# A one-column constant tile widened from 4 to 64 bytes, in an attention and feed-forward block

## The chip, the core and the metric

The kernel runs on one core of a Trainium2 chip. A core has TensorE (PE, matrix multiplication), VectorE (DVE), ScalarE (ACT), GpSimd (POOL) and SyncE (SP, whose queue issues most of the DMAs). Operands stand in SBUF, which has 128 partitions; a tile takes the same byte range of every partition, so that its place is one start address. Results of multiplications go to eight PSUM banks. The metric is device time in microseconds, as the median of several executions.

## The reference

The input x has 2048 rows (tokens) of 1024 columns, in float32. Cut to what matters:

```python
def attn(x):                                   # one head of 256
    q, k, v = split(x @ Wqkv + bqkv)
    p = softmax(q @ k.T / 16)
    return (p @ v) @ Wo + bo

def ffn(x):                                    # 1024 -> 2752 -> 1024
    return (silu(x @ W_gate.T) * (x @ W_up.T)) @ W_down.T

x = x + layernorm(attn(layernorm(x)))
x = x + layernorm(ffn(layernorm(x)))
```

## The kernel before

Every multiplication is done in a split form: an operand is kept as a high and a low half of type float32r, and a product is the sum of three multiplications, high by high, high by low and low by high (mm3, lines 143 to 147, and mmc, lines 601 to 606, which holds line 604). Each loads a 128x128 block of weights from SBUF and streams 512 columns of a moving operand from SBUF past them, into a PSUM bank. The halves are made by split (lines 107 to 109): a cast on ScalarE (L108), then a subtraction on VectorE (L109).

The work goes through these stages.

1. *Projections and layernorm.* Rows of x are loaded by 128 (load_x, L163), normalised, transposed by TensorE against an identity tile called ident (L138) and split into xT, which is the tile xT0 or a2 in turn. qk (lines 184 on) multiplies xT by the weights wqk, and v_block (L205, L206) multiplies xT by the v weights, which are in wvo.
2. *Attention.* For each block of 128 rows: scores (through mm3, q as weights and kx as moving data; q is in qa or qb by turns of four blocks), softmax on ScalarE and VectorE, transposes of the probabilities p_s (turn, L267), the product with v (attend, L275 and L276, both operands in a1 and a2), a transpose of its result (turn_o, L284), the output projection (proj, through mm3, oTs as weights and wvo as moving data), the residual and the transposes for the feed-forward stage (xpose, L346).
3. *Feed forward, gate and up* (gate_up, lines 622 to 690). The tokens are taken in two halves. The products are arranged by a scheme of sums in the manner of Strassen, seven in place of eight. Moving data are the activations in xb, kx, a1, qa and qb. The weights are loaded into raw tiles (f2p, f4_4, wr0), combined on VectorE, split, and held in a ring of slots: four quarters of a2 and two halves of wvo. Which slot a weight gets depends on the order in which slots come free, so the same source line reads its weights from a2 at one time and from wvo at another. In the first half the remaining attention blocks' residual and transposes run as jobs between products.
4. *Feed forward, down* (run_down, run_steps). A slot holds both the weights and the moving data of a step, so that both operands are in a2, or both in wvo.

SBUF is given out from both ends. The pool "const" starts at the left end, at low addresses, and holds ident, the biases, the constant mhalf, the small statistics tiles ys and small, then a1, a2 and the raw tiles f4, f2p and f2_4; the pools "x0", "w", "s" and "xi" (xT0, wr, qb, p_s, oTs, xe, xi) stand behind it on the same side. Pools with side="right" are given out from the high end downwards:

```python
    rpool = pool("right", side="right")
    kx = tl(rpool, [P, 8, 2, 512], F32R, "kx")
    wvo = tl(rpool, [P, 4, 2, 512], F32R, "wvo")
    qa = tl(rpool, [P, 2, 2, 512], F32R, "qa")
```

wqk, xb and x1 are on the right as well. A tile's width in a partition is rounded up to 32 bytes. mhalf holds the exponent -0.5 for the reciprocal square root that GpSimd computes (L120, L804). The tile framework orders the instructions by a simulated timeline and sets the waits between engines.

Of the kernel before, what the change touches and what calls it, by code (L numbers as in the profile page):

```python
# [8 lines left out]
F32 = mybir.dt.float32  # L9
# [6 lines left out]
P = 128  # L16
# [18 lines left out]
def block_kernel(ctx, tc, x, wqk, wv, bqk, bv, wo, bo, wgu, wlast, wd, out):  # L35
# [14 lines left out]
    def pool(name, side=None, **kw):  # L50
        return tc.alloc_tile_pool(name=name, bufs=1, side=side, reuse_waits="tile", **kw)

    def tl(p, shape, dt, name):
        return p.tile(shape, dt, tag=name, name=name, bufs=1)


    cpool = pool("const")
# [2 lines left out]
    bqk_s = tl(cpool, [P, 4], F32, "bqk_s")  # L60
    bv_s = tl(cpool, [P, D], F32, "bv_s")
    bo_s = tl(cpool, [P, C], F32, "bo_s")
    mhalf = tl(cpool, [P, 1], F32, "mhalf")
    nc.vector.memset(mhalf, -0.5)

    ys = [tl(cpool, [P, 32], F32, f"ys{i}") for i in range(2 * TB)]
# [961 lines left out]
```

## Time and profile before

| what | value |
|---|---|
| median of 3 runs | 1729.71 us (1728.43 to 1729.87) |
| profiled execution | 1728.61 us, its span 1726.8 us |
| TensorE clock granted, mean | 0.992 |
| busy: TensorE, weight loads, VectorE, ScalarE, GpSimd | 1699.3, 1393.6, 1091.8, 689.1, 89.0 us |
| multiplications | 7788, 5424 of them at line 604 |
| feed-forward stage | from 454 us to the end of the span |
| DMA | 271.01 MB, 157 GB/s |

A group of the profile is the instructions of one line, engine and set of tiles, with the mean duration of one. Weight loads (PEld) overlap the multiplications. A multiplication's duration runs from its start to its modelled end, and the next starts before that; the distance from one start to the next is what it takes of TensorE's time. In tile names the buffer number is left out, so "a" is a1 or a2 and "f" is one of f4 and f2_4.

### The profile page before, as it was taken

To read this page: it belongs to the slowest core of one execution; us is meant where nothing else is said; L and a number is where in the kernel's file an instruction comes from. 1 tells how busy PE (TensorE), PEld (TensorE's weight loads), DVE (VectorE), ACT (ScalarE), POOL (GpSimd) and SP (SyncE) were. 2 spreads that over 40 slices of the span, in tenths; PEclk is the share of its full clock that TensorE was granted. 3 is DMA by queue.
4 is the path that set the end of the run, shared out by engine and by line. 5 is a ranking of instruction groups with operands and counts; after the bars stand their busy time and mean duration, and the time that the engine had idled before them with its cause. 6 is when DMAs were issued, how large, how long until landed. Compare 5 with 4: busy or idle time off the path is not lost.

```text
span 1726.8 us, 21119 instructions
## 1 busy us (share of the span) xinstructions
PE 1699.3 (98%) x7788; PEld 1393.6 (81%) x7788; DVE 1091.8 (63%) x1666; ACT 689.1 (40%) x1031; POOL 89.0 (5%) x118
## 2 busy tenths in 40 slices
PE   8999999999899999999999999999999999999997
PEld 7888887888688888888888888788888888888886
DVE  8633667667877777676378457866555564345458
ACT  3222445544544444443355444433333333244343
POOL 1000001000011111110000000100000000000001
PEclk8999999999899999999999999999999999999999
DMA  6221023234755566665358655633332223486654
GB/s 210 80 80 37 37 74 125 97 126 172 257 195 195 201 215 214 214 204 190 122 191 255 194 194 193 205 105 113 129 109 94 91 92 122 132 280 195 195 185 159
DMA packets 131015, 271.01 MB, mean 157 GB/s; under 512 B 13280, under 2 KB 29792, under 8 KB 130912
## 3 DMA queue, kind: packets, MB, share of 16 engines
q1 hardware_dynamic: 128176, 262.72, 45.6%
q10 hardware_dynamic: 2736, 6.95, 1.1%
q8 instruction: 61, 1.00, 0.2%
q14 instruction: 42, 0.34, 0.1%
HBM read 185.73 MB, written 83.89 MB: 156 GB/s over the span
## 4 chain that ended last, share of the span: by engine, by line
PE 93%; DVE 3%; DMA 2%; issue 1%; ACT 1%; POOL 0%; SPq 0%; POOLq 0%; DVEq 0%; ACTq 0%
PE bank L604 70%; PE bank L146 4%; PE bank L145 4%; PE bank L147 4%; PE bank L275 3%; PE bank L276 2%; PE bank L267 1%; PE bank L205 1%; PE bank L206 1%; PE bank L346 1%; DMA f<-x 1%; PE bank L138 1%; DVE small L115 0%; PE bank L773 0%; PE bank L774 0%
## 5 line engine op out<-in xcount | busy, mean ns | idle before, releaser
L604 PE MATMUL bank<-a 128*128 128x512 f32 x1176 | 273.8, 390 | 0.0
L604 PEld LDWEIGHTS bank<-a 128*128 128x128 f32 x1176 | 220.8, 188 | 46.8
L604 PE MATMUL bank<-xb,a 128*128 128x512 f32 x816 | 197.3, 395 | 0.0
L109 DVE TENSOR_TENSOR a<-f2p,a 128x1024 fp32r<-128x1024 f32 (+2 forms) x114 | 124.7, 1095 | 93.4 <-ACT a L108 81.0
L617 DVE TENSOR_TENSOR xi<-bank,xi 128x512 f32<-128x512 f32 (+1 forms) x168 | 113.3, 685 | 111.1 <-PE bank L604 70.1
L604 PEld LDWEIGHTS bank<-xb,a 128*128 128x128 f32 x816 | 152.9, 187 | 37.1
L604 PE MATMUL bank<-kx,a 128*128 128x512 f32 x648 | 157.1, 395 | 0.0
L604 PE MATMUL bank<-a,a 128*128 128x512 f32 x648 | 153.4, 390 | 0.0
L108 ACT CAST a<-f2p 128x1024 fp32r<-128x1024 f32 (+2 forms) x114 | 107.6, 949 | 112.5 <-PE bank L604 102.4
L109 DVE TENSOR_TENSOR a<-f,a 128x512 fp32r<-128x512 f32 (+3 forms) x93 | 91.3, 981 | 91.4 <-ACT a L108 88.0
L604 PEld LDWEIGHTS bank<-kx,a 128*128 128x128 f32 x648 | 121.5, 187 | 29.5
L604 PEld LDWEIGHTS bank<-a,a 128*128 128x128 f32 x648 | 121.6, 188 | 26.4
L604 PE MATMUL bank<-wvo 128*128 128x512 f32 x600 | 142.4, 390 | 0.0
L604 PEld LDWEIGHTS bank<-wvo 128*128 128x128 f32 x600 | 112.6, 188 | 24.4
L108 ACT CAST a<-f 128x512 fp32r<-128x512 f32 (+3 forms) x93 | 69.4, 747 | 125.7 <-PE bank L604 90.6
L275 PE MATMUL bank<-a,a 128*128 128x512 f32 x256 | 94.5, 402 | 2.8 <-ACT f L348 2.0
L109 DVE TENSOR_TENSOR wvo<-f2p,wvo 128x1024 fp32r<-128x1024 f32 (+2 forms) x48 | 54.8, 1141 | 66.2 <-ACT wvo L108 57.6
L604 PE MATMUL bank<-a,wvo 128*128 128x512 f32 x384 | 93.7, 396 | 1.2 <-ACT xi L663 1.2
L604 PE MATMUL bank<-kx,wvo 128*128 128x512 f32 x384 | 91.9, 390 | 0.0
L617 DVE TENSOR_TENSOR xi<-xi,xi 128x512 f32<-128x512 f32 x124 | 85.4, 688 | 4.3
L604 PEld LDWEIGHTS bank<-a,wvo 128*128 128x128 f32 x384 | 72.0, 188 | 18.8 <-ACT xi L663 1.6
L604 PEld LDWEIGHTS bank<-kx,wvo 128*128 128x128 f32 x384 | 72.1, 188 | 15.7
(234 smaller groups left out, 2751.2 us busy)
## 6 DMA issues: line engine op xcount, KB each, us to landing
f2p<-wgu SPq DMA_DIRECT2D x43, 512.0 KB, 5.0
hd_S<-xi SPq DMA_DIRECT2D x80, 256.0 KB, 4.6
f<-x SPq DMA_DIRECT2D x30, 512.0 KB, 3.9
hd_A<-xi SPq DMA_DIRECT2D x60, 256.0 KB, 2.0
f<-wgu SPq DMA_DIRECT2D x21, 512.0 KB, 4.4
wr<-wgu SPq DMA_DIRECT2D x20, 512.0 KB, 5.9
f<-wd SPq DMA_DIRECT2D x20, 512.0 KB, 5.0
td_T<-f SPq DMA_DIRECT2D x40, 256.0 KB, 4.5
```

What stands on the lines that cost most here:

```text
L108: nc.scalar.copy(hi, src)
L109: (lo_engine or nc.vector).tensor_tensor(lo, src, f32(hi), ALU.subtract)
L138: nc.tensor.transpose(b[:, j * P : (j + 1) * P], t[:, cb * P : (cb + 1) * P], ident)
L145: nc.tensor.matmul(o, w[0], m[0], start=first, stop=False)
L146: nc.tensor.matmul(o, w[0], m[1], start=False, stop=False)
L147: nc.tensor.matmul(o, w[1], m[0], start=False, stop=last)
L205: nc.tensor.matmul(b, xg[:, c, 0, cols], wv_s[:, c, :, :].rearrange("p a f -> p (a f)"), start=(c == 0), stop=False)
L206: nc.tensor.matmul(b[:, D:], xg[:, c, 1, cols], wv_s[:, c, 0, :], start=False, stop=(c == 7))
L275: nc.tensor.matmul(b, p[:, k, 0, :], vt[:, k, :, :].rearrange("p h d -> p (h d)"), start=(k == 0), stop=False)
L276: nc.tensor.matmul(b[:, D:], p[:, k, 1, :], vt[:, k, 0, :], start=False, stop=(k == NKB - 1))
L604: one = nc.tensor.matmul(o, w[i], m[j], start=first and n == 0, stop=last and n == 2, skip_group_check=chained)
L617: nc.vector.tensor_tensor(o, a, b, op)
```

## The change

The tile mhalf is made 16 columns wide, and its first column is used in its place. It is written and read as before.

```diff
-    mhalf = tl(cpool, [P, 1], F32, "mhalf")
+
+    mhalf = tl(cpool, [P, 16], F32, "mhalf")[:, 0:1]
     nc.vector.memset(mhalf, -0.5)
```

mhalf took 4 bytes, rounded up to 32, and takes 64 now. The tiles given out behind it on the left stand 32 bytes higher; those in front of it, and those on the right, stay. Some start addresses, in bytes within a partition:

| tile | side | before | modulo 64 | after | modulo 64 |
|---|---|---|---|---|---|
| ident | left, ahead of mhalf | 2176 | 0 | 2176 | 0 |
| bo_s | left, ahead of mhalf | 3744 | 32 | 3744 | 32 |
| mhalf | left | 7840 | 32 | 7840 | 32 |
| ys0 | left | 7872 | 0 | 7904 | 32 |
| a1 | left | 9920 | 0 | 9952 | 32 |
| a2 | left | 42688 | 0 | 42720 | 32 |
| f4_0 | left | 75456 | 0 | 75488 | 32 |
| qb | left | 114368 | 0 | 114400 | 32 |
| xb | right | 139232 | 32 | 139232 | 32 |
| kx | right | 172000 | 32 | 172000 | 32 |
| wvo | right | 204768 | 32 | 204768 | 32 |
| qa | right | 221152 | 32 | 221152 | 32 |

The blank line moves every later line number by one: line 604 is line 605 after it.

## The prediction

> **What bounds the kernel now.** I read the busy times first, then the chain that ended last, then the matrix multiplications grouped by the tiles they read, then the timeline of one stretch of the feed-forward stage. A residue below is a tile's start address in its partition modulo 64 bytes. In the built program every left tile from ys0 on has residue 0 before and 32 after; every right tile (kx, wvo, qa, xb, wqk, x1) has 32 in both; ident has 0 in both. A mixed multiplication reads moving data and weights of different residues, an equal one of the same. The tiles' inner steps are multiples of 64 bytes, so a slice has its tile's residue.
>
> ```profile
> PE 1699.3 (98%) x7788; PEld 1393.6 (81%) x7788; DVE 1091.8 (63%) x1666; ACT 689.1 (40%) x1031; POOL 89.0 (5%) x118
> PE 93%; DVE 3%; DMA 2%; issue 1%; ACT 1%; POOL 0%; SPq 0%; POOLq 0%; DVEq 0%; ACTq 0%
> ```
>
> TensorE is busy for 98% of the span and holds 93% of the chain, so nanoseconds on every multiplication reach the end. The groups (number left out of a name: "a" is a1 or a2, weights are in a2 or wvo; columns: line, engine, operation, tiles, tile size, count, busy us, mean ns):
>
> ```profile
> L604 PE MATMUL bank<-a 128*128 128x512 f32 x1176 | 273.8, 390 | 0.0
> L604 PE MATMUL bank<-xb,a 128*128 128x512 f32 x816 | 197.3, 395 | 0.0
> L604 PE MATMUL bank<-kx,a 128*128 128x512 f32 x648 | 157.1, 395 | 0.0
> L604 PE MATMUL bank<-a,a 128*128 128x512 f32 x648 | 153.4, 390 | 0.0
> L604 PE MATMUL bank<-wvo 128*128 128x512 f32 x600 | 142.4, 390 | 0.0
> L604 PE MATMUL bank<-a,wvo 128*128 128x512 f32 x384 | 93.7, 396 | 1.2 <-ACT xi L663 1.2
> L604 PE MATMUL bank<-kx,wvo 128*128 128x512 f32 x384 | 91.9, 390 | 0.0
> ```
>
> Left with left (a; a,a) and right with right (wvo; kx,wvo) take 390; the three that cross take 395 or 396. The code, the shape and the type are the same. Ends of multiplications are modelled, so I check it on starts (start us, us, engine, line, tiles, count):
>
> ```profile
> 501.95 5.77 PE L604 MATMUL bank<-kx,a 128*128 128x512 f32 x24
> 507.56 5.64 PE L604 MATMUL bank<-kx,wvo 128*128 128x512 f32 x24
> 513.04 5.63 PE L604 MATMUL bank<-a,a 128*128 128x512 f32 x24
> 518.51 5.76 PE L604 MATMUL bank<-a,wvo 128*128 128x512 f32 x24
> 524.10 11.36 PE L604 MATMUL bank<-xb,a 128*128 128x512 f32 x48
> 535.30 1.04 PE L346 MATMUL bank<-ident,f 128*128 128x128 f32 x8
> ```
>
> From one start to the next group's start, the mixed 24 + 24 + 48 take 5.61 + 5.59 + 11.20 = 22.40 us, 233.3 ns each; the equal 48 take 10.95 us, 228.1 ns each. A mixed multiplication costs 5.2 ns more, and both equal kinds (0 with 0, 32 with 32) are the cheap ones.
>
> **The change, part by part.** The scheduler's order does not move: each engine has the same instructions with the same waits, in the same places. One memset writes the same single column. All that changes is 32 bytes on the left tiles' addresses, after which left and right both have 32.
>
> *Feed-forward multiplications (L604).* Mixed now: 816 (xb,a), 648 (kx,a), 384 (a,wvo), and outside the rows above 180 (qa,a) and 60 (qb,wvo): 2088. All become equal. At 5.2 ns that is 10.9 us; by the rounded group means (5 to 6 ns) 10.4 to 12.5. I take 10.9. The multiplications that are equal already keep 390: residue 0 (a) and 32 (wvo) both have it.
>
> *Projections to q and k (qk).* 384 multiplications read xT (left) against wqk (right), all mixed, all becoming equal. No equal row of this line exists; its neighbours on the same source lines are the scores, in these rows:
>
> ```profile
> L145 PE MATMUL bank<-kx,qb 128*128 128x512 f32 x64 | 26.5, 415 | 0.0
> L145 PE MATMUL bank<-kx,qa 128*128 128x512 f32 x64 | 26.3, 411 | 0.0
> L147 PE MATMUL bank<-kx,qb 128*128 128x512 f32 x64 | 25.3, 396 | 0.0
> L147 PE MATMUL bank<-a,wqk 128*128 128x512 f32 x64 | 25.3, 395 | 0.0
> L147 PE MATMUL bank<-kx,qa 128*128 128x512 f32 x64 | 25.3, 395 | 0.0
> L346 PE MATMUL bank<-ident,f 128*128 128x128 f32 x112 | 15.5, 272 | 0.0
> ```
>
> Between 0 (as scores with qa, equal, against qb, mixed: 1 ns at L147) and 6 ns: 0 to 2.3 us. The layout of wqk and xT is that of the feed-forward operands and 395 is their mixed mean, so I take 5.2 ns: 2.0 us.
>
> *Scores with qb* (192, becoming equal): 0 to 1.2 us, by the rows about 1 ns: 0.2. *Output projection* (192, oTs left against wvo right): no equal row; 0 to 1.2, taken 1.0 as its contiguous moving operand is nearer to L604's. *v_block* (wvo moving, 128 of 512 and 128 of 256 columns): means of 393 and 282 lie under those of the equal attention products (402 and 286), so I take 0 from 0 to 1.3.
>
> *Transposes: the loss.* ident stays at 0 while every tile transposed against it moves from 0 to 32, so 128 (L138) + 128 (L346) + 256 (L267) + 32 (L284) = 544 equal ones become mixed. No mixed transpose exists before. Bounds: 0, and the 6 ns of a mixed 512-column product, 3.3 us in all. A transpose streams a quarter of the columns but loads as many weights; between those I take half of 5.2 ns: 1.4 us lost. In the stretch above one takes about 109 ns (the eight stand 0.87 us in the chain).
>
> *VectorE, ScalarE, DMA.* Their left operands move too. Rows with both kinds of destination:
>
> ```profile
> L109 DVE TENSOR_TENSOR a<-f2p,a 128x1024 fp32r<-128x1024 f32 x87 | 106.2, 1221 | 92.4 <-ACT a L108 80.5 <-PE bank L604 11.7
> L109 DVE TENSOR_TENSOR wvo<-f2p,wvo 128x1024 fp32r<-128x1024 f32 x41 | 50.0, 1220 | 66.1 <-ACT wvo L108 57.6 <-PE bank L604 8.5
> ```
>
> 1221 with all operands at 0, 1220 when they cross. The casts on ScalarE have 1053 (a) and 1045 (wvo): no price for 32. Loads of x_d into bo_s (residue 32) land in a median 4.3 us and into wr (0) in 4.0; of xT_d in 4.3 and 5.5: no direction, so 0. Were a transfer 0.3 us later, the cover is the ring of raw tiles loaded ahead; uncovered it would show at the start of the feed-forward stage, where the chain holds one load of 5.89 us.
>
> *Sum.* -10.9 - 2.0 - 0.2 - 1.0 + 1.4 = -12.7 us of TensorE time. The feed-forward part passes on: TensorE has 160.00 of 160 us from 775 and 443.47 of 444 from 1122. The front's net 1.8 us may be partly given back where TensorE waits (254.88 of 264 us from 190 to 454); I drop 0.4. That leaves 12.3. The profiled execution took 1728.6 (span 1726.8 and 1.8 around it): 1716.3. It lies 1.1 below the median 1729.7, so as a median 1717.4.
>
> **A rule against it.** The Trainium skill, SBUF — State Buffer, section "Who interferes with whom", gives TensorE two independent read ports, one for the moving operand and one for weight loads, and says TensorE never waits on anyone. By that rule the two operands' addresses could not matter and the sum would be 0. The trace disagrees with 390 against 395 ns.
>
> **Rivals.** (1) *Nothing changes.* The crossing price could belong to the two ends of the memory and not to the residue: in L604 the two always go together before. Then the 2088 still cross ends and keep 395, the transposes stay as they are, and the time is 1729.7. For: the scores show hardly any price. Against: nothing else in the code tells the two ends apart, and 32 bytes are the only difference their addresses share. (2) *The feed binds.* With faster products VectorE (240.59 of 321 us from 454 to 775) and DMA (0.61 there) might set the pace in the first half's gate and up products: eight periods of 108 mixed products (the 96 above and 12 of qa,a) are 4.5 us lost, 1721.9. Against: VectorE idles 25% there, and its waits are for TensorE. (3) *Slower.* A mixed transpose may lose its overlap with the next weight load. It decides at 12.3 + 1.4 = 13.7 us over 544, 25 ns on each of some 109. At 40 ns it costs 21.8 us and the time is 1739. For: weight loads are 81% of the span, short transposes have the least slack around them. Against: the mixed price seen is 5 ns a load, whatever the tile.
>
> **How the numbers follow.** Forecast 0.80, nothing 0.07, feed 0.07, slower 0.06. The unknown terms at their ends give gains of 12.5 + 2.3 + 1.2 + 1.2 + 1.3 = 18.5 (1711) and 10.4 - 3.3 = 7.1 (1722.6). All small terms at one end together is unlikely, so the low end is 1713; the high end is 1722.6, which holds the feed case. Outside are nothing and slower, 0.13, and a little below. About 0.2% (3.5 us) can be told from no change: faster has forecast and feed, 0.87; same 0.07; slower 0.06.
>
> **What would show it.** Right: every L604 group near 390; 24 products of kx,a or a,wvo from start to start in 5.48 us, not 5.6; L147 with wqk near 390; L346 between 272 and 278 ns, eight in 0.87 to 0.92 us; L109 still 1220. Wrong: xb,a and kx,a still at 395 (ends, not residues); xb,a at 390 with new idle time on TensorE released by casts (feed); transposes tens of ns longer (slower); or wvo and kx,wvo risen, if 32 was cheap only beside traffic at 0.

## The result and the profile after

The changed kernel takes 1708.58 us (1707.72 to 1712.36) beside 1729.26 us for the kernel before in the same measurement: a ratio of 0.9888, 95% interval 0.9876 to 0.9900. It is 1.1% faster, 20.7 us. The direction was the one forecast; the gain is 1.7 times the 12.3 us forecast, and the time lies 4.4 us below the low end of the range.

The profiled execution has a span of 1705.9 us, 20.9 less than before. Its busy times and chain by engine:

```profile
PE 1678.0 (98%) x7788; PEld 1393.6 (82%) x7788; DVE 1090.9 (64%) x1666; ACT 690.2 (40%) x1031; POOL 93.4 (5%) x118
PE 95%; DVE 2%; ACT 1%; issue 1%; DMA 1%; POOL 0%; POOLq 0%; DVEq 0%; ACTq 0%; SPq 0%
```

TensorE's busy time fell by 21.3 us, all of the gain; VectorE and ScalarE are within 1.1 us of what they were. The feed-forward groups (line 605 is the line 604 of before):

```profile
L605 PE MATMUL bank<-a 128*128 128x512 f32 x1176 | 272.7, 389 | 0.0
L605 PE MATMUL bank<-xb,a 128*128 128x512 f32 x816 | 192.0, 389 | 0.0
L605 PE MATMUL bank<-kx,a 128*128 128x512 f32 x648 | 152.9, 389 | 0.0
L605 PE MATMUL bank<-a,a 128*128 128x512 f32 x648 | 152.6, 389 | 0.0
L605 PE MATMUL bank<-wvo 128*128 128x512 f32 x600 | 141.5, 389 | 0.0
L605 PE MATMUL bank<-a,wvo 128*128 128x512 f32 x384 | 91.2, 389 | 1.2 <-ACT xi L664 1.2
```

The three crossing groups fell from 395 and 396, as forecast. But the groups that never crossed fell too, from 390 to 389. The starts in the timeline show it better, on the stretch that answers to the one shown before:

```profile
492.40 1.03 PE L347 MATMUL bank<-ident,f 128*128 128x128 f32 x8
493.19 1.62 PE L605 MATMUL bank<-qa,a 128*128 128x512 f32 x6
494.65 1.52 PE L605 MATMUL bank<-qb,a 128*128 128x512 f32 x6
496.01 1.52 PE L605 MATMUL bank<-qa,a 128*128 128x512 f32 x6
497.37 1.52 PE L605 MATMUL bank<-qb,a 128*128 128x512 f32 x6
498.73 5.60 PE L605 MATMUL bank<-kx,a 128*128 128x512 f32 x24
504.17 5.60 PE L605 MATMUL bank<-kx,wvo 128*128 128x512 f32 x24
509.61 5.60 PE L605 MATMUL bank<-a,a 128*128 128x512 f32 x24
515.05 5.60 PE L605 MATMUL bank<-a,wvo 128*128 128x512 f32 x24
520.49 11.05 PE L605 MATMUL bank<-xb,a 128*128 128x512 f32 x48
531.38 1.03 PE L347 MATMUL bank<-ident,f 128*128 128x128 f32 x8
```

Every 24 products now take 5.44 us from start to start, 226.7 ns each, whatever their tiles. Before, mixed ones took 233.3 and equal ones 228.1 in that stretch. So 6.6 ns came off each mixed product, and 1.4 off each equal one.

Taking the distance from each product of line 604 to the start of the multiplication behind it, over the whole trace, these products stand for 1253.1 us before and 1233.9 after: 19.2 of the 20.9 us.

### The profile page after: what moved, and what is told of

Its sections match the earlier page's. It is cut to its first block, busy times and chain, and to the rows that moved or that the text cites. A ratio compares the mean times of both kernels' runs of the same rounds, so it can differ in the third digit from the quotient of the medians.

```text
span 1705.9 us, 21119 instructions
## 1 busy us (share of the span) xinstructions
PE 1678.0 (98%) x7788; PEld 1393.6 (82%) x7788; DVE 1090.9 (64%) x1666; ACT 690.2 (40%) x1031; POOL 93.4 (5%) x118
## 4 chain that ended last, share of the span: by engine, by line
PE 95%; DVE 2%; ACT 1%; issue 1%; DMA 1%; POOL 0%; POOLq 0%; DVEq 0%; ACTq 0%; SPq 0%
PE bank L605 72%; PE bank L147 4%; PE bank L146 4%; PE bank L148 4%; PE bank L276 3%; PE bank L277 2%; PE bank L206 2%; PE bank L268 1%; PE bank L207 1%; PE bank L347 1%; PE bank L139 1%; PE bank L774 0%; DVE small L116 0%; PE bank L775 0%; DMA f<-wv 0%
## 5 line engine op out<-in xcount | busy, mean ns | idle before, releaser
L605 PE MATMUL bank<-xb,a 128*128 128x512 f32 x816 | 192.0, 389 | 0.0
L605 PE MATMUL bank<-kx,a 128*128 128x512 f32 x648 | 152.9, 389 | 0.0
```

Of the source, the lines that this page charges most:

```text
L605: one = nc.tensor.matmul(o, w[i], m[j], start=first and n == 0, stop=last and n == 2, skip_group_check=chained)
```

## The experiments

Two things were open. Which relation between the addresses has the price: that the two operands come from the two ends of SBUF, that they differ modulo 64, or modulo something larger? And why did the equal products get faster? In the experiments, "place" is a start address modulo 256; left tiles (a1, a2, f, qb, xT0) have 192 before and 224 after, right tiles 224 in both. Where a kernel's edit is shown, it is against the kernel before, but for the one on the changed kernel below.

**The right side moved in place of the left.**

```diff
     qa = tl(rpool, [P, 2, 2, 512], F32R, "qa")
+    tl(rpool, [P, 8], F32, "pad")
```

> The kernel before with a 32-byte tile put behind qa at the right end, so that wvo, kx, qa, xb, wqk and x1 move down by 32 bytes to residue 0; the left side stays at 0. Residue theory (a price where moving data and weights differ modulo 64): all pairs are equal, 1708 us within 2, every L604 group at 389. Theory of the two ends: the groups that cross keep 395, 1729 us. Theory that residue 32 on the left side is what helps (its casts, subtractions and DMAs): the left side has not moved, 1729 us.

Measured 1708.31 us, ratio 0.9874 (0.9858 to 0.9890): the whole gain, with the left side where it was.

```profile
L605 PE MATMUL bank<-xb,a 128*128 128x512 f32 x816 | 192.0, 389 | 0.0
L605 PE MATMUL bank<-a,wvo 128*128 128x512 f32 x384 | 91.2, 389 | 1.2 <-ACT xi L664 1.2
```

Operands still cross from one end to the other and cost nothing more, so the ends are not the cause. Nor is it the left side's place for casts and DMAs, which did not move. What counts is how the two operands stand to each other.

**Part of the right side moved.**

```diff
     kx = tl(rpool, [P, 8, 2, 512], F32R, "kx")
+    tl(rpool, [P, 8], F32, "pad")
     wvo = tl(rpool, [P, 4, 2, 512], F32R, "wvo")
```

> The kernel before with a 32-byte tile between kx and wvo: kx, xb and wqk move to residue 0, wvo and qa stay at 32, the left side stays at 0. Residue theory: kx,a and xb,a (1464 products) fall to 390, kx,wvo and xb,wvo (672) rise to 395; of the 2088 mixed ones 1296 are left. The change took 18 us off 2088, 8.8 ns each with all that follows from one, so 792 fewer give 7 us, and qk, now equal, some 2 us: 1720 us, between 1717 and 1723. Theory of the two ends: kx,wvo stays at 390, kx,a at 395, 1729 us.

Measured 1719.30 us, ratio 0.9941 (0.9926 to 0.9956), inside what the residue theory gave. The timeline, same stretch:

```profile
499.70 5.61 PE L605 MATMUL bank<-kx,a 128*128 128x512 f32 x24
505.15 5.76 PE L605 MATMUL bank<-kx,wvo 128*128 128x512 f32 x24
510.75 5.61 PE L605 MATMUL bank<-a,a 128*128 128x512 f32 x24
516.20 5.76 PE L605 MATMUL bank<-a,wvo 128*128 128x512 f32 x24
521.79 11.05 PE L605 MATMUL bank<-xb,a 128*128 128x512 f32 x48
532.68 1.03 PE L347 MATMUL bank<-ident,f 128*128 128x128 f32 x8
```

kx,a went down to 5.45 us for 24 and kx,wvo up to 5.60: the price followed the addresses from one group to the other. The 48 of xb,a, which come after a mixed run, take 10.89.

**The left side 64, 96 and 160 bytes higher.** In the kernel before, mhalf is widened further, to 24 columns as below (left64), to 32 (left96) or to 48 (left160):

```diff
-    mhalf = tl(cpool, [P, 1], F32, "mhalf")
+    mhalf = tl(cpool, [P, 24], F32, "mhalf")[:, 0:1]
```

> mhalf 96 bytes wide: the left side stands 64 bytes above the kernel before, residue 0 again, and at a multiple of 128. Residue theory modulo 64: as the kernel before, 1729 us, crossing groups at 395. If moving the left side off its old place is what counts, or a modulus of 128 with some other pairing: 1708 us or something between.

Measured 1728.89 us, ratio 1.0002 (0.9993 to 1.0011): the kernel before again. A move alone brings nothing.

> mhalf 128 bytes wide: the left side stands 96 bytes above the kernel before; left and right are equal modulo 64 (32) and differ modulo 128 (32 on the left, 96 on the right). Residue theory modulo 64: 1708 us, all L604 groups at 389. Modulus 128 or more: the crossing groups at 395 and 1729 us.

Measured 1725.38 us, ratio 0.9982 (0.9973 to 0.9991). This broke the theory of 64 bytes, and with it the rule that the change was described by: all tiles behind mhalf and on the right are equal modulo 64, and nearly the whole price is still there.

```profile
L604 PE MATMUL bank<-xb,a 128*128 128x512 f32 x816 | 197.4, 395 | 0.0
L604 PE MATMUL bank<-kx,a 128*128 128x512 f32 x648 | 157.2, 395 | 0.0
L604 PE MATMUL bank<-a,wvo 128*128 128x512 f32 x384 | 92.2, 392 | 1.1 <-ACT xi L663 1.1
```

a,wvo, where the moving operand stands 64 above the weights modulo 256, has 392; the two where it stands 64 below have 395.

> mhalf 192 bytes wide: the left side stands 160 bytes above the kernel before, so that left and right are equal modulo 64 and modulo 128 and differ by 128 modulo 256. If the period is 128 bytes: all L604 groups at 389 and 1708 us. If it is 256 bytes or more: the crossing groups keep a price, and the time lies between that of left96 (1725) and that of the kernel before (1729).

Measured 1727.02 us, ratio 0.9988 (0.9979 to 0.9998). Equal modulo 128 is not enough either: xb,a, kx,a and a,wvo have 395.

**The left side 288 bytes higher,** with 80 columns for mhalf, beside the changed kernel once more:

> mhalf 320 bytes wide: the left side stands 256 bytes above the changed kernel, so that left and right are now equal modulo 512 too, where in the changed kernel they differ by 256. If the period is 256 bytes: the same as the changed kernel, 1708.6 us, L604 at 389. If the changed kernel still pays something for the 256: lower, by up to the 5 ns of 2088 products, 1698 us.

> The changed kernel itself, beside the next two. 1708.6 us within 1.5 by every theory.

Measured 1708.84 us, ratio 0.9889 (0.9872 to 0.9906), and 1708.34 for the changed kernel, ratio 0.9885 (0.9867 to 0.9903): no difference. In the changed kernel left and right differ by 256 modulo 512, here by nothing, so 256 bytes are a whole period.

**Shifts below 32 bytes.** In the changed kernel, xb and kx are views into slightly wider tiles, xb 16 bytes above the common place and kx 8 below:

```diff
+    tl(rpool, [P, 48], F32, "pad")
-    kx = tl(rpool, [P, 8, 2, 512], F32R, "kx")
+    kx = tl(rpool, [P, 8200], F32R, "kx")[:, 6:6 + 8192].rearrange("p (c h n) -> p c h n", h=2, n=512)
...
-    xb = tl(xpool, [P, 8, 2, 512], F32R, "xb")
+    xb = tl(xpool, [P, 8200], F32R, "xb")[:, 4:4 + 8192].rearrange("p (c h n) -> p c h n", h=2, n=512)
```

> The changed kernel with xb 16 bytes above the place modulo 256 that left, wvo and qa share, and kx 8 bytes below it; wqk 32 above it. Theory that the two streams must stand at the same byte: xb,a, xb,wvo, kx,a and kx,wvo (2136 products) all at 395, 1726 to 1729 us. Theory of whole 32-byte units: xb stays in the unit and keeps 389, kx (1032 products) leaves it and has 395, about 1719 us. Theory that only shifts of 32 bytes or more count: both at 389, and only qk's 2 us, 1710 us.

Measured 1723.82 us, ratio 0.9972 (0.9962 to 0.9981), between two of the forecasts, and the rows decide:

```profile
L605 PE MATMUL bank<-xb,a 128*128 128x512 f32 x816 | 196.1, 394 | 0.0
L605 PE MATMUL bank<-kx,a 128*128 128x512 f32 x648 | 156.4, 394 | 0.0
L605 PE MATMUL bank<-a,wvo 128*128 128x512 f32 x384 | 91.4, 390 | 0.3 <-ACT xi L664 0.3
```

Both shifted tiles pay 5 ns, and a,wvo, which was not shifted, does not. Eight bytes are enough; there is no unit of 32 bytes inside which a shift is free. The time is lower than that theory's 1726 to 1729 because these two shifts cost 4.9 and 5.3 ns a product against 226.7, not the 6.6 of a shift by 32.

The distance from one start to the next, over all of the L604 products that are followed within 250 ns. The difference is the moving operand's place minus that of the weights that are loaded while it streams, which are those of the next product:

| difference modulo 256 | kernel | mean ns |
|---|---|---|
| 0, all products | changed | 226.7 |
| 0, the equal ones among mixed | before | 228.0 |
| 16 | fine | 231.6 |
| 248 (8 below) | fine | 232.0 |
| 32 | before | 233.3 |
| 224 (32 below) | before | 233.4 |
| 64 | left96 | 229.3 |
| 128 | left160 | 232.8 |
| 192 (64 below) | left96 | 233.1 |

**Only qa out of place,** to see whether a mixed product delays its neighbours:

```diff
     wvo = tl(rpool, [P, 4, 2, 512], F32R, "wvo")
+    tl(rpool, [P, 8], F32, "pad")
     qa = tl(rpool, [P, 2, 2, 512], F32R, "qa")
```

> The kernel before with the 32-byte tile between wvo and qa: everything at one place modulo 256 except qa, whose 240 products in L604 (runs of 6, between runs of 6 with qb, which is at the common place) are mixed. If a mixed product delays only itself, 240 times 6.6 ns are 1.6 us and qb,a stays at 392 as after the change, 1.36 us from start to start of 6; time 1710. If a switch upsets the next products too, qb,a rises towards the 399 of before and its six towards 1.39 us, and the time is 1711 to 1712.

Measured 1711.57 us, ratio 0.9902 (0.9887 to 0.9916). The timeline:

```profile
495.24 1.65 PE L605 MATMUL bank<-qa,a 128*128 128x512 f32 x6
496.72 1.55 PE L605 MATMUL bank<-qb,a 128*128 128x512 f32 x6
498.11 1.56 PE L605 MATMUL bank<-qa,a 128*128 128x512 f32 x6
499.51 1.55 PE L605 MATMUL bank<-qb,a 128*128 128x512 f32 x6
500.89 5.60 PE L605 MATMUL bank<-kx,a 128*128 128x512 f32 x24
506.33 5.60 PE L605 MATMUL bank<-kx,wvo 128*128 128x512 f32 x24
```

qb and a2 stand at the same place, yet six of qb,a take 1.39 and 1.38 us where the changed kernel has 1.36: the runs of qa beside them slow them down. Further off, 24 of kx,a take 5.44, as they do undisturbed. So a mixed product upsets the next few, and that is what the equal products of the kernel before paid. In that kernel's trace the first product behind a run of such disturbed ones is on average some 5 ns above 226.7, the fourth 5.5, the seventh 2.0 and from the ninth on none (sorted as in the table). The down stage shows the same with a single switch between slots:

```profile
1566.65 5.63 PE L604 MATMUL bank<-wvo 128*128 128x512 f32 x24
1572.13 11.07 PE L604 MATMUL bank<-a 128*128 128x512 f32 x48
1583.04 5.63 PE L604 MATMUL bank<-wvo 128*128 128x512 f32 x24
```

These are lines of the kernel before. 24 take 5.48 us and 48 take 10.91; after the change the same runs take 5.44 and 10.88:

```profile
1546.46 5.60 PE L605 MATMUL bank<-wvo 128*128 128x512 f32 x24
1551.90 11.04 PE L605 MATMUL bank<-a 128*128 128x512 f32 x48
1562.78 5.60 PE L605 MATMUL bank<-wvo 128*128 128x512 f32 x24
```

The excess is 0.04 and 0.03 us for 24 and for 48 products: a price of one switch, not of each product.

None of these products is mixed: a product's own two operands are both in a2 or both in wvo. What crosses at the switch is a load. At the one at 1572.13 us the kernel before shows

```profile
1571.67 0.62 PE L604 MATMUL bank<-wvo 128*128 128x512 f32 x2
1571.90 0.19 PEld L604 LDWEIGHTS bank<-a 128*128 128x128 f32 x1
```

The second of the two products starts at 1571.89 us, and the load of the next product's weights, the first from a, begins 4 ns later and runs beside it. That product takes 235 ns to the next start. Over the 56 switches of this kind the last product before the switch takes 234.6 ns before the change and 226.6 after it. The stages with mixed products agree. Of the equal products that stand right before a mixed one, with eight equal ones ahead of them, 40 run while weights from another place are loaded and take 235.0 ns; 19 run beside a load from their own place, since only the moving tile changes, and take 226.7. So the price goes by the place of the moving operand against that of the weights loaded meanwhile, and not against that of the product's own weights. It need not fall on that product: at the same switches in left96, which is described above, the last product takes 226 ns and those behind it pay, 14 ns in all where the moving operand stands 64 above the weights loaded and 38 where it stands 64 below.

**ident moved as well,** first by 32 bytes with the edit below (ident32), then, with a pad of 24 columns and mhalf at 56, to the common place modulo 256 (ident224):

```diff
+    tl(cpool, [P, 8], F32, "pad")
     ident = tl(cpool, [P, P], F32, "ident")
```

> The kernel before with a 32-byte tile ahead of ident: ident moves to residue 32 too, and everything behind it stands as in the changed kernel. If a mixed transpose has a price, the 544 get it back: L139, L268 and L347 fall by up to 2.6 ns and the time by up to 1.4 us, 1707. If transposes pay nothing for it: the same as the changed kernel, 1708.6.

> As left288, but 96 of the 288 bytes are put ahead of ident, so that ident too stands at the common place modulo 256 (224); it is 64 off in the kernel before, 96 off in the changed one and 64 off in ident32. If a transpose pays for an identity at another place modulo 256, the 544 get that back: up to 2.6 ns each, 1.4 us, and the next products some tails, 1706 us. If not: as left288.

Measured 1709.85 us, ratio 0.9892 (0.9877 to 0.9907), and 1707.84 us, ratio 0.9884 (0.9868 to 0.9899). Neither can be told from the changed kernel. The rows of L347 and L268 in ident224 are what they are in the changed kernel:

```profile
L268 PE MATMUL bank<-ident,p_s 128*128 128x128 f32 x256 | 39.0, 273 | 0.7 <-ACT p_s L259 0.6
L347 PE MATMUL bank<-ident,f 128*128 128x128 f32 x112 | 15.5, 272 | 0.0
```

A transpose pays nothing that these rows show for an identity at another place. The row of L139 can't decide it: its mean is 277 in ident224, but 288 and 275 in two profiles of the same changed kernel (after and again).

## Why the prediction was wrong

The mechanism was right in kind (the places of the two operands, not the ends of the memory), and its size was not. Its period was wrong too, 64 bytes where the runs show 256; that this change makes the places equal by either was luck. The step that failed for the time is the term for the feed-forward multiplications, 10.9 us at 5.2 ns over 2088 products, which measured 19.2 us.

- *The mixed products.* 5.2 ns was the distance from 233.3 to 228.1, the equal products of the kernel before. I took those for undisturbed. They were not: they held the tails of the mixed ones beside them, and of the switches between slots. Against the undisturbed 226.7 ns the price is 6.6, and 2088 of them are 13.8 us.
- *The equal products,* which were to keep 390. They did not keep it: 228.0 went to 226.7, and 1.3 ns over 3336 are 4.3 us. With the 13.8 that makes 18.1 of the 19.2 us; the rest lies in distances over 250 ns, which these means leave out. The upper bound fell for the same reason: 12.5 us came from rounded means of 395 and 396 against a contaminated 390, and did not count tails at all.
- *qk,* 2.0 us. The six rows of xT and a against wqk fell by 4 to 6 ns each (a,wqk at the last of the three lines from 395 to 390); 5 ns over 384 are 1.9. Right.
- *Scores and output projection,* 0.2 and 1.0 us. The rows of kx,qb fell by 1 to 3 ns and those of wvo,oTs by 2 to 3: about 0.4 each. The sum is right within the noise, the projection's share was too high.
- *v_block,* taken at 0. Its products of 512 columns with a went from 393 to 398 and those of 256 from 282 to 280, so a pair lost about 3 ns, 0.4 us over 128. I had left a loss out there. It is not equality that costs: with the moving operand 32 below the weights, in left64, the two rows have 398 and 281 as well. Only the 32 above of the kernel before, which kx_xb has here too (393 and 282), is cheaper in this pattern.
- *Transposes,* 1.4 us lost. Measured 272 and 272 (L346, now L347), 273 and 273 (L267, now L268), 286 and 288 (L138, now L139). The step was mistaken twice: they pay no price that shows (but for L138, which varies by more than that between profiles of one kernel), and by the period of 256 they were never equal before, since ident stood at 128 and the tiles at 192.
- *VectorE, ScalarE, DMA,* 0. Right: the subtraction into a has 1220 (1221 before), the cast 1054 (1053).
- *What passes on.* I dropped 0.4 us for waits. TensorE's busy time fell by 21.3 and the span by 20.9, which is the same size; where it was given back is not shown. The measured terms, 19.2 + 1.9 + 0.8 - 0.4, make 21.5 beside these 21.3.

Of the rivals, *nothing changes* fell with the result, and its mechanism (the two ends) with right0. *The feed binds* did not happen: the 168 products of a period on the chain went from 38.91 us to 38.10, 226.8 each, in the stretch for which the rival was set up. *Slower* did not happen, since no transpose lost its overlap. (Its price was summed wrongly: 21.8 us lost against 13.7 gained give 1737.8 us from 1729.7; the 1739 holds the forecast's 1.4 for transposes beside the 21.8.) The rule of the Trainium skill (SBUF — State Buffer, "Who interferes with whom") by which the two reads of TensorE are independent does not hold for these products: the same products take 226.7 ns or up to 233.4, by nothing but the operands' places.

What caused the residue rule to look right is a coincidence of the kernel: before, left and right differ by 32 bytes modulo 256 as well, so that a period of 64, 128 or 256 fits that trace. The mixed price alone could not tell them apart; left96 and left160 did.

One thing stays open: why the two read streams disturb each other, and with a period of 256 bytes, is not shown by any run. The prediction paired each moving operand with the weights of its own product. In this kernel these nearly always have the place of those loaded meanwhile, so its count of 2088 was not far off; the price at the slot switches of the down stage, where it saw none, is what this pairing missed.

## What to carry to other kernels

Where TensorE is the bound and loads new weights for every product of 512 columns, start the moving operands and the weights, in all of the slots that take turns, at the same byte modulo 256; a few bytes of padding in a constant tile did it here for 1.1%. All of these runs are in float32r; no other type was tried. When two groups of a trace differ by a few nanoseconds, compare them with the cheapest undisturbed instance, not with the average of the cheap group: neighbours may carry part of the price. And a rule that fits one pair of addresses needs a second pair before its period is believed.

## What the runs showed of the hardware that was not expected

- With moving data and weights at one place modulo 256, a product of 128x512 in float32r takes 226.7 ns from start to start with hardly any spread; at another place 229.3 to 233.4. Differences of 8, 16, 32, 64 and 128 bytes all cost; 256 costs nothing (left288 against the changed kernel, 1708.84 and 1708.34 us).
- The weights that matter are those loaded while a product streams. One product beside a load from another place takes 8 ns more, and with the five to seven after it some 31 ns (the mean over the slot switches of the feed-forward down stage, before).
- The price need not be symmetric: in left96 64 above costs 2.6 ns, 64 below 6.4. At 32 it is the same both ways, 233.3 and 233.4 ns.
- Where products of 512 and of 256 columns take turns (v_block), a moving operand 32 above the weights was about 3 ns a pair cheaper than equal places or 32 below.
